# A graph layer with gathered rows: a window's rows of x transposed on chip, an explicit bound on each gather, and the first list and the final flag moved forward

## The chip, the cores and the metric

The kernel runs on one core of one Trainium2 chip. The metric is the device time of one execution in microseconds (us). Ten runs of the kernel before have a median of 24131.06 us. Five engines work side by side: PE (TensorE, matrix products), DVE (VectorE), ACT (ScalarE), POOL (GpSimd) and SP (SyncE). SP, ACT and POOL also issue DMA transfers.

## The reference

```python
src, dst = (edge_index[0], edge_index[1])
Xs = X[src]
m_data = Xs @ W_data.T + b_data
m_ctrl = Xs @ W_control.T + b_control
msg = jnp.where((edge_types == 0)[:, None], m_data, m_ctrl)
agg = jax.ops.segment_sum(msg, dst, num_segments=X.shape[0])
out = agg + (X @ W_self.T + b_self)
return jax.nn.relu(out)
...
x = _layernorm(x + _L0_gnn_ref(...), axis=-1)
```

There are 50,000 nodes with 128 features in float32 and 1,650,000 edges, sorted by their destination; each node has an edge to itself among them. An edge's type chooses one of two weight matrices. The output is the layer normalization, without scale or shift, of x plus the rectified sum.

## The kernel before

**Sums first, weights later.** Edges of one type with the same destination can be summed before the weights are applied. So the kernel sums rows of x by destination and type, and multiplies the sums with the weights once for each destination.

**Blocks.** The edges are cut into 503 blocks (`NBLK`), about 3,284 edges each. A block writes into a window of 112 nodes (`B`) that begins at a base read from the data. Most of its edges come as 24 chunks of 128 edges (2 steps `Q` with 12 chunks `R` each). Edges from a node to itself are left out of the chunks and their places are filled with other edges of the block (`fill`, L300 to L330, on DVE); such an edge's own row is added from the window's x, transposed (`left_out_rows`, L358 to L361). Another 128 edges of a block are fetched one row at a time (`single_rows`, L428 to L443).

**A block on the engines.** POOL gathers the 24 chunks: each is one indirect DMA of 128 rows of x (L464), six to a buffer and ten buffers (`SLOTS`). SP and ACT fetch the 128 single rows, 64 each in two batches of 32: an engine first loads 32 addresses into registers (L435) and then issues 32 DMAs of one row of 512 bytes (L440). DVE compares the edges' columns with 0 to 119 and so makes a matrix of ones and zeros for each chunk (`onehot`, L401) and counts them (L409). PE multiplies each chunk of rows with its matrix into a sum in PSUM (L483); after the twelfth chunk of a step it adds the single rows (L489), for which it waits once a block (`rows_fetched`, L446 to L451), and the counts for the bias (L492). DVE adds the step's result into the window's sums (L499) and begins the next window with the overlap (L512).

**The end of a block.** `layer` (L514) multiplies the window's x, transposed (`xT`), with the self weights (L517), and adds bias (L518) and weighted sums (L520), all into one PSUM tile `po`. `moments` (L523) takes the rectified `po` plus the window's rows of x (`xw`), then mean and variance on DVE. `root` (L532) is one square root on ACT, `store` (L537) normalizes and issues the output's DMA on SP (L543).

**Loads of the window.** Three blocks ahead, `window` (L390) loads the base of the block into a register of SP (L387) and loads the window's rows of x twice: as they are (`xw`, L393, 112 rows of 512 bytes) and transposed from a transposed copy in memory (`xT`, L395).

**Order.** The schedule is written out by hand: the loop at L566 goes over the blocks, and each engine's queue follows the order of its statements. `single_rows` is two blocks ahead (`AHEAD`), `fill` five (`RAHEAD`). Every ten blocks the next group's lists of edges are loaded (`load_edges`, L156 to L170). In a block SP's order is: the base, `xw`, `xT`, 32 addresses, 32 rows, the output of an earlier block, 32 addresses, 32 rows.

**Start and end.** The weights are loaded and transposed one after the other through two buffers (L905 to L911); after them `idx0`, the list for the first block's gathers, is loaded (L116). DVE copies the column numbers into PSUM (L127) before the list of ones (L130) from which POOL makes a triangle (L133). After the last block, DVE and PE work out from collected minima and maxima whether the data kept the assumptions of this path (L615 to L640); the flag is read by all engines, and a general path follows if it is set. With these inputs it is not set.

Of the kernel before, what the change touches and what calls it, by code (L numbers as in the profile page):

```python
# [11 lines left out]
F32 = mybir.dt.float32  # L12
# [4 lines left out]
ALU = mybir.AluOpType  # L17
AX = mybir.AxisListType
SP = mybir.EngineType.SP
# [3 lines left out]
N = 50000  # L23
D = 128
ROW = 4 * D
E = 1650000
P = 128
# [7 lines left out]
W = 60  # L35
Q = 2
PASS = 6
B = 112
C = R * Q
F = 42  # L40
S = 64
# [4 lines left out]
NBLK = 2 + (E - C * CH) // BE  # L46
# [7 lines left out]
AHEAD = 2  # L54
# [30 lines left out]
def straight(ctx, tc, c, x, x_t, src_t, dst_t, etype_t, src_f, dst_f, etype_f, src_x, dst_first, first_p, out):  # L85
# [13 lines left out]
    nc = tc.nc  # L99
    keep = ctx.enter_context(tc.tile_pool(name="keep", bufs=1))  # L100
# [6 lines left out]
    stp = ctx.enter_context(tc.tile_pool(name="stp", bufs=3))  # L107
# [3 lines left out]
    ps_o = ctx.enter_context(tc.tile_pool(name="ps_o", bufs=1, space=bass.MemoryType.PSUM))  # L111
# [7 lines left out]
    num = keep.tile([P, 2 * W], F32, name="num")  # L119
# [75 lines left out]
    base_i = keep.tile([1, BL], I32, name="base_i")  # L195
# [172 lines left out]
    def column(k):  # L368
        return k // R * R1 + k % R
# [11 lines left out]

    idxs = {0: idx0}
    bys, pcs, zs, pls, bases, ats, ys = {}, {}, {}, {}, {}, {}, {}
    ohs, cnts, accs, xws, xTs, pos, hs, mvs, sds = {}, {}, {}, {}, {}, {}, {}, {}, {}

    def base_of(b):
        return nc.values_load(base_i[0:1, b:b + 1], engines=[SP], min_val=0, max_val=N - B,  # L387
                              skip_runtime_bounds_check_because="it was clamped to this")

    def window(b):  # L390
        at = bases[b] = base_of(b)
        xw = stp.tile([B, D], F32, name="xw", bufs=5)
        nc.sync.dma_start(xw, x[bass.ds(at, B), :])  # L393
        xT = stp.tile([P, B], F32, name="xT", bufs=5)
        nc.sync.dma_start(xT, x_t[:, bass.ds(at, B)])  # L395
        xws[b], xTs[b] = xw, xT

    def onehot(b):
        g, i = divmod(b, GB)
# [13 lines left out]

    ROW_SLOTS = AHEAD + 2
    TURN = S // 2
    LOAD = TURN // 1
# [11 lines left out]
    def single_rows(b, q, part):  # L428

        if q == 0 and part == 0:  # L430
            ys[b] = stp.tile([S, Q, D], F32, name="yx", bufs=ROW_SLOTS)
        both = []
        for j, (eng, dma) in enumerate(((SP, nc.sync), (ACT, nc.scalar))):
            at = j * TURN + part * LOAD
            _, rows = nc.values_load_multi_w_load_instructions(  # L435
                ats[b][0:1, q * S + at:q * S + at + LOAD], engines=[eng], **RANGE)
            both.append([(dma, fetched[j][b % ROW_SLOTS], at + k, row) for k, row in enumerate(rows)])
        for pair in zip(*both):
            for dma, sem, k, row in pair:
                copy = dma.dma_start(ys[b][k:k + 1, q, :].bitcast(U8), x_bytes[:, bass.ds(row, ROW)])  # L440
# [17 lines left out]
    def gathers(b, ks):  # L458
        i = pass_no[0] % SLOTS
        pass_no[0] += 1  # L460
        y = gat.tile([P, PASS, D], F32, name="y")
        for k in ks:
            r = LAST if b == NBLK - 1 and k == RCH - 1 else P
            copy = nc.gpsimd.indirect_dma_start(  # L464
                out=y[:r, k % PASS, :], out_offset=None, in_=x,
                in_offset=bass.IndirectOffsetOnAxis(ap=idxs[b][:r, column(k):column(k) + 1], axis=0))
# [46 lines left out]

    def layer(b):  # L514
        a = sums[b % RING]
        po = ps_o.tile([B, D], F32, name="po")
        nc.tensor.matmul(po, xTs.pop(b), c["wselfT"], start=True, stop=False)  # L517
        nc.tensor.matmul(po, a[0:3, 2, :B], bias, start=False, stop=False)  # L518
        for t in range(2):
            nc.tensor.matmul(po, a[:, t, :B], c["wmsgT"][:, t * D:(t + 1) * D], start=False, stop=t == 1)  # L520
        pos[b] = po
# [15 lines left out]
    def store(b):  # L537
# [4 lines left out]
        nc.vector.tensor_scalar(o, hs.pop(b), mv[:, 0:1], rstd, op0=ALU.subtract, op1=ALU.mult)  # L542
        nc.sync.dma_start(out[bass.ds(bases.pop(b), B), :], o)  # L543

    for b in range(1, AHEAD + 1):
        offsets(b)
    columns(0)
# [6 lines left out]
    for b in range(1, RAHEAD):  # L554
        fill(b)
        left_out_columns(b)
        left_out_matrix(b)
        if b < AHEAD:
            onehot(b)
            counts(b)  # L560
            for q in range(Q):
                for part in range(1):
                    single_rows(b, q, part)
        if b == 1:
            clear_sums()
    for b in range(NBLK + 1):  # L566
        if b + 3 < NBLK:
            window(b + 3)
        g, i = divmod(b, GB)
# [11 lines left out]
        for q, (step, ks) in enumerate(passes_of(b)):  # L581
# [27 lines left out]
                left_out_matrix(b + RAHEAD)  # L609
                offsets(b + AHEAD + 1)  # L610
            if q % 2 == 0 and not plain(b + AHEAD):
                single_rows(b + AHEAD, q // 2, 0)


    ones = keep.tile([P, 1], F32, name="ones")  # L615
    nc.vector.memset(ones, 1.0)
    mm = keep.tile([P, 2], F32, name="mm")
    nc.vector.tensor_reduce(mm[:, 0:1], stats[:, :, 0, :], AX.XY, ALU.min)
    nc.vector.tensor_reduce(mm[:, 1:2], stats[:, :, 1, :], AX.XY, ALU.max)
    bad = keep.tile([P, 3], F32, name="bad")  # L620
    least = keep.tile([P, 1], F32, name="least")
    nc.vector.tensor_reduce(least, loops, AX.X, ALU.min)
    nc.vector.tensor_scalar(bad[:, 2:3], least, float(F), None, op0=ALU.is_lt)
    nc.vector.tensor_scalar(bad[:, 0:1], mm[:, 0:1], 0.0, None, op0=ALU.is_lt)
    nc.vector.tensor_scalar(bad[:, 1:2], mm[:, 1:2], float(W), None, op0=ALU.is_ge)
    gap = keep.tile([1, 3], F32, name="gap")
    nc.vector.tensor_reduce(gap[:, 0:1], shift, AX.X, ALU.min)
    nc.vector.tensor_reduce(gap[:, 1:2], shift, AX.X, ALU.max)
    nc.vector.tensor_scalar(gap[:, 0:1], gap[:, 0:1], 0.0, None, op0=ALU.is_lt)
    nc.vector.tensor_scalar(gap[:, 1:2], gap[:, 1:2], float(B), None, op0=ALU.is_gt)  # L630
    pb = ps_o.tile([B, D], F32, name="po")
    nc.tensor.matmul(pb[:3, 0:1], bad, ones, start=True, stop=True)
    both = keep.tile([3, 1], F32, name="both")
    nc.vector.tensor_copy(both, pb[:3, 0:1])
    pc = ps_o.tile([B, D], F32, name="po")
    nc.tensor.matmul(pc[:1, 0:1], both, ones[:3, 0:1], start=True, stop=True)
    nc.vector.tensor_copy(gap[:, 2:3], pc[:1, 0:1])
    total = keep.tile([1, 1], F32, name="total")
    nc.vector.tensor_reduce(total, gap, AX.X, ALU.add)
    nc.vector.tensor_copy(c["bad"], total)  # L640


def general(ctx, tc, c, x, src, dst, etype, out):
# [221 lines left out]
def gnn_resnorm(  # L865
# [109 lines left out]
```

## Time and profile before

| What | Value |
|---|---|
| Ten runs, median | 24131.06 us |
| Ten runs, lowest and highest | 24106.23 and 24138.2 us |
| Profiled execution, its own time | 24112.32 us |
| Profiled execution, span of its instructions | 24110.6 us |
| Busy share of the span | PE 29%, weight loads 26%, DVE 44%, ACT 1%, POOL 47% |
| DMA traffic | 970.58 MB in 753,406 packets, 40 GB/s on average |
| Issues | 32,064 single rows on SP and as many on ACT; 12,061 gathers on POOL; 503 each of `xw`, `xT` and the output on SP |

Busy times leave out the instructions that set registers, wait, or issue DMAs, so SP has no busy time of its own; its issues stand in the timeline as SPq, those of ACT as ACTq. A group's row in the profile gives line, engine, operation and tiles, then the number of instructions, the busy time in us, the mean of one in ns, and the engine's idle time just before them with what ended most of it. PEq is a wait in PE's sequencer.

### The profile page before, as it was taken

The page shows a single profiled execution, that of the slowest core. Times are in us where ns is not written, and L with a number is a line of the kernel's source. Part 1 is how long each engine was busy: PE and PEld are TensorE (multiplying, and loading weights), DVE is VectorE, ACT ScalarE, POOL GpSimd, SP SyncE. Part 2 cuts the span into 40 slices and gives each one's busy share as a digit, 9 for nine tenths or more (in the row PEclk, how much of TensorE's full clock was granted, in tenths as well). Part 3 has the DMA queues.
Part 4 walks back from the last instruction along what each step waited for, and adds up shares of the span by engine and source line. Part 5 has one row for each costly group of instructions (what it writes and reads, how often), then busy time and mean ns, then how long its engine had stood idle before and what let it go on. Part 6 is the DMA issues. An engine that isn't in the chain of part 4 may idle for free. (4 is left out here: it accounts for less than half of the span.)

```text
span 24110.6 us, 243274 instructions
## 1 busy us (share of the span) xinstructions
PE 7060.2 (29%) x34836; PEld 6353.7 (26%) x34837; DVE 10668.4 (44%) x13316; ACT 151.6 (1%) x509; POOL 11419.1 (47%) x12071
## 2 busy tenths in 40 slices
PE   2322322222232222322222222322223222232222
PEld 2222222222222222222222222222222222222222
DVE  5444444444444444444444444444444444444443
ACT  0000000000000000000000000000000000000000
POOL 5444444444444444444444444444444444444444
PEclk6555555555555555555555555555555555555555
DMA  1111111111111111111111111111111111111111
GB/s 44 41 41 39 40 41 41 39 40 41 40 40 40 41 40 40 40 40 41 39 41 40 41 40 40 40 40 40 40 40 41 40 40 41 40 40 41 41 39 37
DMA packets 753406, 970.58 MB, mean 40 GB/s; under 512 B 355316, under 2 KB 552099, under 8 KB 751778
## 3 DMA queue, kind: packets, MB, share of 16 engines
q0 software_dynamic: 385968, 791.19, 11.5%
q1 hardware_dynamic: 301244, 146.99, 2.3%
q10 hardware_dynamic: 64566, 16.74, 0.3%
q14 instruction: 1344, 11.01, 0.1%
q8 instruction: 284, 4.65, 0.1%
HBM read 924.76 MB, written 29.02 MB: 40 GB/s over the span
## 5 line engine op out<-in xcount | busy, mean ns | idle before, releaser
L464 POOL DMA_INDIRECT y<-in_x,idx x12048 | 11405.2, 947 | 12592.8 <-PE acc L483 7743.9
L499 DVE TENSOR_TENSOR sums<-acc,sums 128x180 f32 x1006 | 348.1, 346 | 11144.5 <-PE acc L492 10707.6
L483 PE MATMUL acc<-oh,y 128*128 128x120 f32 x24122 | 5098.2, 398 | 3.5 <-issue 3.5
L483 PEld LDWEIGHTS acc<-oh,y 128*128 128x128 f32 x24122 | 4860.5, 307 | 4.0 <-issue 4.0
L489 PE MATMUL acc<-oh,yx 64*128 64x120 f32 x2004 | 635.7, 408 | 11442.5 <-PEq L449 11301.1
L489 PEld LDWEIGHTS acc<-oh,yx 64*128 64x128 f32 x2004 | 401.7, 249 | 11632.5 <-PEq L449 11416.1
L409 DVE TENSOR_REDUCE cnt<-oh 128x240 bf16<-128x3120 f32 x503 | 2934.2, 5833 | 0.1
L401 DVE TENSOR_TENSOR oh<-col,small 128x3120 f32<-128x3120 f32 x503 | 1695.9, 3371 | 0.0
L336 PE MATMUL small<-ones_b,by 128*84 128x1 bf16 x501 | 115.9, 231 | 5319.4 <-DVE by L329 3157.5
L336 PEld LDWEIGHTS <-by 128*84 128x84 bf16 x501 | 73.3, 146 | 5386.9 <-DVE by L329 3197.1
L329 DVE TENSOR_REDUCE by<-old 128x84 bf16<-128x1092 f32 x501 | 1062.9, 2122 | 18.8 <-DVE old L326 1.4
L525 DVE SCALAR_TENSOR_TENSOR h<-po,xw 112x128 f32<-112x128 f32 x503 | 146.9, 292 | 1650.7 <-PE po L520 1470.0
L310 DVE TENSOR_TENSOR m<-rk,small 128x1092 f32<-128x1092 f32 x501 | 647.3, 1292 | 17.5 <-DVE small L308 0.5
L313 DVE TENSOR_TENSOR new<-m,small 128x1092 f32<-128x1092 f32 x501 | 647.0, 1291 | 17.2
L317 DVE TENSOR_REDUCE v_new<-new 128x26 f32<-128x1092 f32 x501 | 646.9, 1291 | 17.2
L326 DVE TENSOR_TENSOR old<-m,small 128x1092 f32<-128x1092 f32 x501 | 643.5, 1284 | 0.0
L520 PE MATMUL po<-wmsgT,sums 128*112 128x128 f32 x2012 | 525.6, 407 | 0.0
L520 PEld LDWEIGHTS po<-wmsgT,sums 128*112 128x112 f32 x2012 | 382.1, 261 | 110.7 <-issue 94.7
L518 PE MATMUL po<-bias,sums 3*112 3x128 f32 x1006 | 353.7, 448 | 9.8 <-DVE sums L499 8.0
L517 PE MATMUL po<-wselfT,xT 128*112 128x128 f32 x1006 | 315.5, 417 | 0.0
L534 ACT ACTIVATE sd<-mv,eps 112x1 f32<-112x1 f32 x503 | 148.3, 295 | 23768.2 <-issue 22066.2
L512 DVE TENSOR_TENSOR sums<-pl,sums 128x336 f32<-128x336 f32 x501 | 254.4, 508 | 84.6 <-issue 74.8
(115 smaller groups left out, 3673.3 us busy)
## 6 DMA issues: line engine op xcount, KB each, us to landing
yx<-in_x ACTq DMA_DIRECT2D x32064, 0.5 KB
yx<-in_x SPq DMA_DIRECT2D x32064, 0.5 KB
y<-in_x,idx POOLq DMA_INDIRECT x12048
xw<-in_x SPq DMA_DIRECT2D x503, 56.0 KB
xT<-in_x_t SPq DMA_DIRECT2D x503, 56.0 KB
out<-o SPq DMA_DIRECT2D x503, 56.0 KB
vf_all<-vd SPq DMA_DIRECT2D x51, 420.0 KB
s<-in_src_t SPq DMA_DIRECT2D x51, 130.0 KB
```

What stands on the lines that cost most here:

```text
L310: nc.vector.tensor_tensor(m, rk_g[g][:, i, :, None].to_broadcast([P, C1, F]), rank_no_ps[:, None, :].to_broadcast([P, C1, F]), op=ALU.is_e ...
L313: nc.vector.tensor_tensor(new.rearrange("p (q r) f -> p q r f", r=R1), m.rearrange("p (q r) f -> p q r f", r=R1), vf.rearrange("p (q f) -> ...
L317: nc.vector.tensor_reduce(v, new, AX.X, ALU.add)
L326: nc.vector.tensor_tensor(old, m, cb[:, :, None].to_broadcast([P, C1, F]), op=ALU.mult)
L329: nc.vector.tensor_reduce(by, old.rearrange("p (q r) f -> p q f r", r=R1), AX.X, ALU.add)
L401: nc.vector.tensor_tensor(oh, col_g[g][:, i, :, None].to_broadcast([P, C1, 2 * W]), num_ps[:, None, :].to_broadcast([P, C1, 2 * W]), op=AL ...
L409: nc.vector.tensor_reduce(cnt, ohs[b].rearrange("p (q r) w -> p q w r", r=R1), AX.X, ALU.add)
L464: copy = nc.gpsimd.indirect_dma_start(out=y[:r, k % PASS, :], out_offset=None, in_=x, in_offset=bass.IndirectOffsetOnAxis(ap=idxs[b][:r, c ...
L483: nc.tensor.matmul(acc[:, :2, :].rearrange("p t w -> p (t w)"), y[:r, k % PASS, :], ohs[b][:r, column(k), :], start=k == of_step[0], stop= ...
L489: nc.tensor.matmul(acc[:, :2, :].rearrange("p t w -> p (t w)"), ys[b][:, q, :], ohs[b][:S, q * R1 + R, :], start=False, stop=True)
L518: nc.tensor.matmul(po, a[0:3, 2, :B], bias, start=False, stop=False)
L520: nc.tensor.matmul(po, a[:, t, :B], c["wmsgT"][:, t * D:(t + 1) * D], start=False, stop=t == 1)
```

## The change

The window's rows of x are no longer loaded. PE transposes `xT` into the second half of the PSUM tile `po`, and DVE copies that half to `h` and adds the rectified half to it. SP loads the bases of five blocks at once. Each gather carries a bound for its indices, 49,999. The weights get three buffers in SBUF and PSUM each, and these SBUF buffers stay allocated. The copy of the column numbers stands after the list of ones and the triangle. The flag's work is moved ahead of the last block's. `single_rows` loses an argument that had one value only. Line numbers from L129 on shift by a few: the gather becomes L465, its product L485, the single rows L441, the row product L491, `xT`'s load L397, the transpose L520, the copy L530.

```diff
-    nc.vector.tensor_copy(num_ps, num)
 ...
     nc.gpsimd.affine_select(out=below, in_=ones_b, pattern=[[1, P]], compare_op=ALU.is_gt, fill=0.0,
                             base=0, channel_multiplier=-1)
+    nc.vector.tensor_copy(num_ps, num)
...
-    def base_of(b):
-        return nc.values_load(base_i[0:1, b:b + 1], engines=[SP], min_val=0, max_val=N - B,
-                              skip_runtime_bounds_check_because="it was clamped to this")
+    BASES = 5

     def window(b):
-        at = bases[b] = base_of(b)
-        xw = stp.tile([B, D], F32, name="xw", bufs=5)
-        nc.sync.dma_start(xw, x[bass.ds(at, B), :])
+        if b % BASES == 0:
+            n = min(BASES, NBLK - b)
+            _, regs = nc.values_load_multi_w_load_instructions(
+                base_i[0:1, b:b + n], engines=[SP], min_val=0, max_val=N - B,
+                skip_runtime_bounds_check_because="it was clamped to this")
+            bases.update({b + i: at for i, at in enumerate(regs)})
+        at = bases[b]
         xT = stp.tile([P, B], F32, name="xT", bufs=5)
         nc.sync.dma_start(xT, x_t[:, bass.ds(at, B)])
-        xws[b], xTs[b] = xw, xT
+        xTs[b] = xT
...
             copy = nc.gpsimd.indirect_dma_start(
                 out=y[:r, k % PASS, :], out_offset=None, in_=x,
-                in_offset=bass.IndirectOffsetOnAxis(ap=idxs[b][:r, column(k):column(k) + 1], axis=0))
+                in_offset=bass.IndirectOffsetOnAxis(ap=idxs[b][:r, column(k):column(k) + 1], axis=0),
+                bounds_check=N - 1)
...
     def layer(b):
         a = sums[b % RING]
-        po = ps_o.tile([B, D], F32, name="po")
-        nc.tensor.matmul(po, xTs.pop(b), c["wselfT"], start=True, stop=False)
+        both = ps_o.tile([B, 2, D], F32, name="po")
+        po, xT = both[:, 0, :], xTs.pop(b)
+        nc.tensor.transpose(both[:, 1, :], xT, c["ident"])
+        nc.tensor.matmul(po, xT, c["wselfT"], start=True, stop=False)
...
     def moments(b):
         h = stp.tile([B, D], F32, name="h")
-        nc.vector.scalar_tensor_tensor(h, pos.pop(b), 0.0, xws.pop(b), op0=ALU.max, op1=ALU.add)
+        po = pos.pop(b)
+        nc.vector.tensor_copy(h, po[:, 1, :])
+        nc.vector.scalar_tensor_tensor(h, po[:, 0, :], 0.0, h, op0=ALU.max, op1=ALU.add)
...
     for b in range(NBLK + 1):
+        if b == NBLK - 1:
+            find_bad()
...
-    with tc.tile_pool(name="wts", bufs=2) as wts, \
-            tc.tile_pool(name="wts_ps", bufs=2, space=bass.MemoryType.PSUM) as wts_ps:
-        for w, o in ((w_data, wmsgT[:, :D]), (w_ctrl, wmsgT[:, D:]), (w_self, wselfT)):
-            w_sb = wts.tile([P, D], F32, name="w_sb")
+    w_all = const.tile([P, 3, D], F32, name="w_all")
+    with tc.tile_pool(name="wts_ps", bufs=3, space=bass.MemoryType.PSUM) as wts_ps:
+        for i, (w, o) in enumerate(((w_data, wmsgT[:, :D]), (w_ctrl, wmsgT[:, D:]), (w_self, wselfT))):
+            w_sb = w_all[:, i, :]
```

`find_bad` is the block of statements of L615 to L640 as a function, with its two small products in the first half of a `po` tile.

More of the change, by code (lines that the diff above doesn't have):

```diff
@@ L383, in straight @@
     bys, pcs, zs, pls, bases, ats, ys = {}, {}, {}, {}, {}, {}, {}
-    ohs, cnts, accs, xws, xTs, pos, hs, mvs, sds = {}, {}, {}, {}, {}, {}, {}, {}, {}
-    def base_of(b):
-        return nc.values_load(base_i[0:1, b:b + 1], engines=[SP], min_val=0, max_val=N - B,
-                              skip_runtime_bounds_check_because="it was clamped to this")
+    ohs, cnts, accs, xTs, pos, hs, mvs, sds = {}, {}, {}, {}, {}, {}, {}, {}
+    BASES = 5
     def window(b):
-        at = bases[b] = base_of(b)
-        xw = stp.tile([B, D], F32, name="xw", bufs=5)
-        nc.sync.dma_start(xw, x[bass.ds(at, B), :])
+        if b % BASES == 0:
[5 more added lines that the diff above has]
+        at = bases[b]
         xT = stp.tile([P, B], F32, name="xT", bufs=5)
         nc.sync.dma_start(xT, x_t[:, bass.ds(at, B)])
-        xws[b], xTs[b] = xw, xT
+        xTs[b] = xT
     def onehot(b):
@@ L415, in straight @@
     TURN = S // 2
-    LOAD = TURN // 1
     RANGE = dict(min_val=0, max_val=(N - 1) * ROW, skip_runtime_bounds_check_because="where a node's row is")
@@ L426, in offsets, with single_rows @@
             nc.vector.tensor_scalar(ats[b], one_g[g][:, i * X:(i + 1) * X], float(ROW), None, op0=ALU.mult)
-    def single_rows(b, q, part):
-        if q == 0 and part == 0:
+    def single_rows(b, q):
+        if q == 0:
             ys[b] = stp.tile([S, Q, D], F32, name="yx", bufs=ROW_SLOTS)
@@ L433, in single_rows @@
         for j, (eng, dma) in enumerate(((SP, nc.sync), (ACT, nc.scalar))):
-            at = j * TURN + part * LOAD
+            at = j * TURN
             _, rows = nc.values_load_multi_w_load_instructions(
-                ats[b][0:1, q * S + at:q * S + at + LOAD], engines=[eng], **RANGE)
+                ats[b][0:1, q * S + at:q * S + at + TURN], engines=[eng], **RANGE)
             both.append([(dma, fetched[j][b % ROW_SLOTS], at + k, row) for k, row in enumerate(rows)])
@@ L520, in layer @@
             nc.tensor.matmul(po, a[:, t, :B], c["wmsgT"][:, t * D:(t + 1) * D], start=False, stop=t == 1)
-        pos[b] = po
+        pos[b] = both
     def moments(b):
         h = stp.tile([B, D], F32, name="h")
-        nc.vector.scalar_tensor_tensor(h, pos.pop(b), 0.0, xws.pop(b), op0=ALU.max, op1=ALU.add)
+        po = pos.pop(b)
+        nc.vector.tensor_copy(h, po[:, 1, :])
+        nc.vector.scalar_tensor_tensor(h, po[:, 0, :], 0.0, h, op0=ALU.max, op1=ALU.add)
         st = stp.tile([B, 6], F32, name="st")
@@ L543, in store, with find_bad @@
         nc.sync.dma_start(out[bass.ds(bases.pop(b), B), :], o)
+    def find_bad():
+        ones = keep.tile([P, 1], F32, name="ones")
+        nc.vector.memset(ones, 1.0)
+        mm = keep.tile([P, 2], F32, name="mm")
+        nc.vector.tensor_reduce(mm[:, 0:1], stats[:, :, 0, :], AX.XY, ALU.min)
+        nc.vector.tensor_reduce(mm[:, 1:2], stats[:, :, 1, :], AX.XY, ALU.max)
+        bad = keep.tile([P, 3], F32, name="bad")
+        least = keep.tile([P, 1], F32, name="least")
+        nc.vector.tensor_reduce(least, loops, AX.X, ALU.min)
+        nc.vector.tensor_scalar(bad[:, 2:3], least, float(F), None, op0=ALU.is_lt)
+        nc.vector.tensor_scalar(bad[:, 0:1], mm[:, 0:1], 0.0, None, op0=ALU.is_lt)
+        nc.vector.tensor_scalar(bad[:, 1:2], mm[:, 1:2], float(W), None, op0=ALU.is_ge)
+        gap = keep.tile([1, 3], F32, name="gap")
+        nc.vector.tensor_reduce(gap[:, 0:1], shift, AX.X, ALU.min)
+        nc.vector.tensor_reduce(gap[:, 1:2], shift, AX.X, ALU.max)
+        nc.vector.tensor_scalar(gap[:, 0:1], gap[:, 0:1], 0.0, None, op0=ALU.is_lt)
+        nc.vector.tensor_scalar(gap[:, 1:2], gap[:, 1:2], float(B), None, op0=ALU.is_gt)
+        pb = ps_o.tile([B, 2, D], F32, name="po")[:, 0, :]
+        nc.tensor.matmul(pb[:3, 0:1], bad, ones, start=True, stop=True)
+        both = keep.tile([3, 1], F32, name="both")
+        nc.vector.tensor_copy(both, pb[:3, 0:1])
+        pc = ps_o.tile([B, 2, D], F32, name="po")[:, 0, :]
+        nc.tensor.matmul(pc[:1, 0:1], both, ones[:3, 0:1], start=True, stop=True)
+        nc.vector.tensor_copy(gap[:, 2:3], pc[:1, 0:1])
+        total = keep.tile([1, 1], F32, name="total")
+        nc.vector.tensor_reduce(total, gap, AX.X, ALU.add)
+        nc.vector.tensor_copy(c["bad"], total)
     for b in range(1, AHEAD + 1):
@@ L561, in straight @@
             for q in range(Q):
-                for part in range(1):
-                    single_rows(b, q, part)
+                single_rows(b, q)
         if b == 1:
@@ L611, in straight @@
             if q % 2 == 0 and not plain(b + AHEAD):
[L612 to L640, printed above, removed]
+                single_rows(b + AHEAD, q // 2)
 def general(ctx, tc, c, x, src, dst, etype, out):
```

## The prediction

> **What bounds the kernel now.** I read the engines' shares first (the page's first part), then the longest idle times among the costly groups, then SyncE's own waits, then SyncE's order of time.
>
> ```profile
> PE 7060.2 (29%) x34836; PEld 6353.7 (26%) x34837; DVE 10668.4 (44%) x13316; ACT 151.6 (1%) x509; POOL 11419.1 (47%) x12071
> ...
> L464 POOL DMA_INDIRECT y<-in_x,idx x12048 | 11405.2, 947 | 12592.8 <-PE acc L483 7743.9
> ...
> L489 PE MATMUL acc<-oh,yx 64*128 64x120 f32 x2004 | 635.7, 408 | 11442.5 <-PEq L449 11301.1
> ```
>
> No engine is busy half of the time. PE stands still 11,301 us in front of L489, and what ends that is L449, its wait for the single rows of x that SP and ACT fetch (L440). The gathers in turn wait for PE to free a buffer. So everything waits for the single rows. SP's waits are next (us in total, times, longest):
>
> ```profile
> SPq L435 <- DVE sums L499: 445.3, 402, 1.9
> SPq L292 <- DVE cb L273: 15.2, 1, 15.2
> ```
>
> Under 2% of the span: SP waits for nobody, it is always issuing. Its order of time over one block in the middle, and over a block at the end, where no gather is left:
>
> ```profile
> 12001.35 0.32 SPq L393 DMA_DIRECT2D xw<-in_x  x1
> 12001.86 0.36 SPq L395 DMA_DIRECT2D xT<-in_x_t  x1
> 12004.56 22.19 SPq L440 DMA_DIRECT2D yx<-in_x  x32
> 12028.23 0.02 SPq L543 DMA_DIRECT2D out<-o  x1
> 12030.42 18.98 SPq L440 DMA_DIRECT2D yx<-in_x  x32
> 12050.34 0.32 SPq L393 DMA_DIRECT2D xw<-in_x  x1
> ...
> 24054.15 0.32 SPq L393 DMA_DIRECT2D xw<-in_x  x1
> 24054.65 0.36 SPq L395 DMA_DIRECT2D xT<-in_x_t  x1
> 24057.05 10.68 SPq L440 DMA_DIRECT2D yx<-in_x  x32
> 24067.99 0.34 SPq L543 DMA_DIRECT2D out<-o  x1
> 24070.57 10.24 SPq L440 DMA_DIRECT2D yx<-in_x  x32
> 24081.08 15.10 SPq L543 DMA_DIRECT2D out<-o  x4
> ```
>
> The same 32 issues take 22.2 and 19.0 us beside gathers and 10.7 and 10.2 us without. L393 runs 503 times from 28.7 to 24054.0 us: a block takes 47.86 us. The block without gathers takes 24081.08 - 24054.15 = 26.9 us, plus 0.54 for the base load (L387) that this stretch lacks: 27.5 us. So SP's instructions alone are 27.5 us of a block, and the 24 gathers of a block cost SP 20.4 us in stalls. A gather starts every 1.25 us in a run (12006.14, 12007.39, 12008.65), 30.0 us in a block: SP loses 0.68 us for each us in which POOL gathers. ACT, with as many rows, has slack: its load for the first rows starts at 12019.31, 10.7 us after its last issue, when DVE has made the offsets.
>
> A rule of the Trainium skill speaks against this reading and against the change: "DMA: Bandwidth & Descriptors", section "Issuing engines are not separate DMA queues", says that what a sequencer spends on starting DMAs is usually small beside the transfers. By it, an issue less on SP is worth nothing, and the sum below would be -6 us. Here the row differs: the software queue holds 11.5% of the DMA engines and SP's queue 2.3%, while SP issues without a pause. I follow the row.
>
> **The change part by part.**
>
> SP, per block. The xw load goes: one L393 DMA, its address and its register move. What the trace answers for the two lines (durations in ns: least, median, most):
>
> ```profile
> L393 SPq FUSED_REGOPS  x503: 3/37/1397, 28.7 to 24054.0; - x168
> L393 SPq MOVE xw<-in_x x503: 3/29/726, 28.8 to 24054.1; - x168
> L393 SPq DMA_DIRECT2D xw<-in_x x503: 3/322/737, 29.0 to 24054.2; - x168
> ...
> L387 SPq TENSOR_LOAD <-base_i x503: 3/539/1422, 28.3 to 24053.4; - x168
> ```
>
> From xw's issue to xT's is 0.50 us in both places shown; I take 0.50. The base load goes in four blocks of five. The fifth loads five values: 32 values (L435) take 1.868 us and one takes 0.539, so 0.043 for each more, 0.71 us for five. Saved: (503 x 0.54 - 101 x 0.71)/503 = 0.40 us. Together 0.90 us unhindered. Some of these meet stalls (maxima of 1.4 us against a median of 0.04 to 0.54), so 0.90 is a low side and about 1.15 the high one; I take 1.0. All of it is on the path, since SP never waits: 503 x 1.0 = -503 us. SP also gets 144 more semaphore instructions (1,219 against 1,075 in the built programs, 17 ns each in the rows): 2 us in all. They are waits for transfers issued blocks before, so I cost them at nothing; were they late, each would hold the rows queued behind it.
>
> PE. One transpose a block, ahead of L517's product, same operand: half of L517's two records, 0.42 us. It delays the six products behind the layer, whose end frees the buffer for the block's second run of gathers; POOL's 2.90 us gap there (2.8 to 2.9 in every block that I looked at, ended by po L520) becomes about 3.3. That moves gathers, it adds none, and POOL stands still another 15 to 17 us before the next block's first. Nothing; if POOL were the bound, 503 x 0.42 = 211 us.
>
> DVE. A copy of 112x128 out of PSUM, like L525 with 0.292 us, put between the layer and L525, which loses its wait on xw's DMA. Behind it stand the moments, the next one-hot (L401) and the counts; then DVE waits 22 to 24 us for PE at L499. Hidden there; uncovered it would be 503 x 0.32 = 161 us.
>
> POOL. Each gather now carries its bound in a register: 12,061 register moves, one ahead of each gather, and a comparison inside. The trace of before has neither.
> - The move: nearest row L440's MOVE, 29 ns, 0.06 us to the next start. POOL's own semaphore instructions (17 ns) stand between gathers, and the gap stays 0.30 us with one as without; in the rows some of them run before the gather ahead has ended. Bounds 0 and 0.06 us; I take 0.01, nearer the row of the same engine. 24 x 0.01 x 0.68 = 0.16 us a block, +82 us.
> - The comparison: nearest row L464 itself, 947 ns for 128 indices, 7.4 ns each. No page of the skill states a price. If it is done for many indices at once, nothing; if it adds a tenth per index, 0.095 us a gather, 24 x 0.095 x 0.68 = 1.55 us a block, +780 us; a fifth, +1,560. A gain isn't excluded either, should the unbounded form take a longer way: -0.05 us would be -410. I take 0, since the 947 ns hardly vary (941 to 947 up to the median) and look like set-up more than like a loop over indices, and keep the other ends.
>
> The gathers keep their addresses and their bytes, so their stalls of SP stay.
>
> Once-only parts. The weights get three buffers of their own, so the first list (SP's L116, issued at 6.01 us behind the weights' loads and transposes) goes out at about 1 us, and all of SP's start with it: -5 us. DVE's copy of num goes behind the list of ones: it waited 5.4 us for POOL's iota, at the same start, and is inside these 5. The flag's 3.0 us of DVE (L616 to L640, 24095.76 to 24098.78) go ahead of the last block, where DVE waited 3.82 us in one place and 18 in another; the last products may then start a us later, and the tail after the last store loses up to 3: -1 us.
>
> Sum: the profiled execution took 24112.3 us (span 24110.6). 24112.3 - 503 + 82 - 6 = 23,685. The median of the ten runs is 18.8 us above the profiled one, so 23,704; I say 23,700 (-1.8%).
>
> **The rivals.**
>
> The bound costs time inside the gather, and it is slower. Place: L465 on POOL, 24 times a block. From 0.061 us a gather (1.0 / (24 x 0.68)) it eats all that SP saves. At a tenth of 947 ns the time is 23,700 - 82 + 780 = 24,400, at a fifth 25,180. For it: 24 of them a block, in the unit that sets SP's stalls, and 7.4 ns for an index leaves no room for a scalar comparison. Against it: longer pauses between transfers might let SP through more often, so that 0.68 is too much; at half of it, 24,010 for a tenth.
>
> The stalls take what is freed. If a block's time is set by what the gathers and rows occupy together and not by SP's own instructions, 0.9 us less of SP's work is filled with stalls: no change, 24,125. For it: SP and ACT are held at the same times. Against it: ACT, held as much, still has 10.7 us to spare, and the block without gathers falls to 27.5 us.
>
> The gain is larger: a gather with a bound is shorter by 0.05 us, or 56 KB less to fetch per block thins the stalls: 23,300. For it nothing but that no row excludes it.
>
> **How the numbers follow.** The forecast has 0.58, with 23,550 to 23,850 as its own range (0.7 to 1.2 us a block, the move between 0 and 0.02 us). The dearer gather has 0.29: 0.01 that it eats only part of the gain, 0.02 that it just cancels it, 0.26 that it costs more, a third of that beyond 24,650. The stalls that fill up have 0.05 (0.03 no change, 0.02 a little slower by the gathers' moves), the larger gain 0.08. Leaving out the far end of the dear gather and part of the larger gain, the range is 23,350 to 24,650. About 0.2%, 48 us, is what a measurement of this kernel can tell from no change. Faster: 0.58 + 0.08 + 0.01 = 0.67. Same: 0.02 + 0.03 = 0.05. Slower: 0.26 + 0.02 = 0.28.
>
> **What would show it.** Right: the period of the xT issue (L397) near 46.9 us; PE's idle time before the row product still ended by its wait for single rows, some 500 us less; the gather at 947 ns, 1.25 to 1.26 us from start to start. Wrong: a gather group with a mean over 1,010 ns; a gap between gathers over 0.30 us by more than the move; SP batches that last longer than 19 to 22 us; SP waiting in front of xT or out; POOL or DVE without their long waits for PE.

## The result, and the profile after

The changed kernel takes 23331.82 us in the median, the kernel before, run beside it, 24126.78 us. The ratio is 0.9672, 95% interval [0.9664, 0.9681]: 795 us less, or 1.58 us for each of 503 blocks. The time lies 18 us below the low end of the predicted range, 23,350, and 372 us below the 23,704 of the prediction's sum.

Runs were taken in sets, each with the kernel before beside the changed ones. The kernel before took 23,795 to 24,127 us (medians) in some sets and 15,119 to 15,147 us in others, and a kernel is compared only with the runs of before in its own set. The comparison above, and the profile that the prediction was made from, belong to the long ones; I call them stalled sets, for a reason that the timelines show.

The lines of the page after that answer to those shown of before:

```profile
PE 6996.6 (30%) x35339; PEld 6307.2 (27%) x35340; DVE 10832.6 (46%) x13819; ACT 151.4 (1%) x509; POOL 12219.5 (52%) x12071
...
L465 POOL DMA_INDIRECT y<-in_x,idx x12048 | 12204.8, 1013 | 11046.5 <-PE acc L485 6570.7
...
L491 PE MATMUL acc<-oh,yx 64*128 64x120 f32 x2004 | 633.9, 406 | 10699.0 <-PEq L450 10667.1
```

The gather has become longer, 1013 ns against 947: 12,048 of them are 800 us more of POOL. And yet PE's idle time in front of the row product, still ended by its wait for the single rows, is 634 us less (11,301 to 10,667). What bound the kernel still does, but PE waits less for it. SP's own waits (us in total, times, longest) are 0.65 us a block, where the 445 us of before were 0.89:

```profile
SPq L436 <- DVE sums L501: 328.2, 194, 2.3
SPq L292 <- DVE cb L273: 15.4, 1, 15.4
```

For the rest SP is still issuing. Its order of time in the middle and at the end:

```profile
12021.69 0.36 SPq L397 DMA_DIRECT2D xT<-in_x_t  x1
12024.26 20.62 SPq L441 DMA_DIRECT2D yx<-in_x  x32
12045.59 0.00 SPq L549 DMA_DIRECT2D out<-o  x1
12047.78 19.57 SPq L441 DMA_DIRECT2D yx<-in_x  x32
12068.36 0.36 SPq L397 DMA_DIRECT2D xT<-in_x_t  x1
...
23296.15 0.36 SPq L397 DMA_DIRECT2D xT<-in_x_t  x1
23298.74 10.58 SPq L441 DMA_DIRECT2D yx<-in_x  x32
23309.57 0.34 SPq L549 DMA_DIRECT2D out<-o  x1
23312.16 10.25 SPq L441 DMA_DIRECT2D yx<-in_x  x32
23322.69 17.70 SPq L549 DMA_DIRECT2D out<-o  x4
```

The 503 issues of `xT` run from 24.8 to 23296.2 us: a block takes 46.36 us, where it was 47.86. The last block, which has no gather beside it, takes 26.54 us from `xT` to the last stores, and a fifth of the load of five bases (1.327 us in the median) belongs to it: 26.8 us of SP's own work, against 27.5. So 0.7 of the 1.5 us are SP's own work as such a block shows it. What a block takes beyond that (stalls, the short waits, and a tenth of the loads that come every ten blocks) is 20.4 us before and 19.6 now, although POOL gathers longer.

Two or three batches of a timeline are a small sample: single batches of 32 rows take from 10 to over 50 us. So I also worked out the mean over all 1,002 batches of SP in each trace, from the start of the first row's issue to the end of the last one's. It is 19.73 us before and 19.89 now. The rows themselves have not become faster; what has become shorter is the rest of SP's block, 47.86 - 2 x 19.73 = 8.4 us before and 46.36 - 2 x 19.89 = 6.6 now.

POOL's own order of time:

```profile
12044.94 1.01 POOL L465 DMA_INDIRECT y<-in_x,idx  x1 [2.14 <-PE po L524]
12046.26 1.01 POOL L465 DMA_INDIRECT y<-in_x,idx  x1 [0.30 <-issue]
12047.58 1.01 POOL L465 DMA_INDIRECT y<-in_x,idx  x1 [0.30 <-issue]
```

A gather now starts every 1.32 us instead of every 1.25. The gap of 0.30 us is unchanged; what has grown is the gather itself.

### The profile page after: what moved, and what is told of

Read it like the earlier page. It is cut to its first block, busy times and chain, and to the rows that moved or that the text cites. A ratio compares the mean times of both kernels' runs of the same rounds, so it can differ in the third digit from the quotient of the medians.

```text
span 23346.2 us, 254666 instructions
## 1 busy us (share of the span) xinstructions
PE 6996.6 (30%) x35339; PEld 6307.2 (27%) x35340; DVE 10832.6 (46%) x13819; ACT 151.4 (1%) x509; POOL 12219.5 (52%) x12071
## 4 chain that ended last, share of the span: by engine, by line
SPq 55%; issue 34%; DVE 6%; PE 3%; DMA 2%; another core or an unknown queue 0%; ACTq 0%; PEldq 0%; DVEq 0%; ACT 0%
SPq L441 46%; SPq L436 6%; DVE cnt L411 2%; DMA yx<-in_x 2%; SPq L549 2%; PE acc L485 1%; PE acc L491 1%; SPq L397 0%; DVE m L310 0%; DVE new L313 0%; DVE v_new L317 0%; DVE old L326 0%; PE po L524 0%; DVE by L329 0%
## 5 line engine op out<-in xcount | busy, mean ns | idle before, releaser
L465 POOL DMA_INDIRECT y<-in_x,idx x12048 | 12204.8, 1013 | 11046.5 <-PE acc L485 6570.7
L485 PE MATMUL acc<-oh,y 128*128 128x120 f32 x24122 | 4983.3, 391 | 13.2 <-issue 13.1
L485 PEld LDWEIGHTS acc<-oh,y 128*128 128x128 f32 x24122 | 4740.7, 300 | 11.2 <-issue 10.9
L491 PE MATMUL acc<-oh,yx 64*128 64x120 f32 x2004 | 633.9, 406 | 10699.0 <-PEq L450 10667.1
L491 PEld LDWEIGHTS acc<-oh,yx 64*128 64x128 f32 x2004 | 402.4, 249 | 10876.9 <-PEq L450 10774.7
L530 DVE COPY h<-po 112x128 f32<-112x128 f32 x503 | 146.8, 292 | 1806.2 <-PE po L524 1644.7
```

The costliest lines, as they stand in the source:

```text
L465: copy = nc.gpsimd.indirect_dma_start(out=y[:r, k % PASS, :], out_offset=None, in_=x, in_offset=bass.IndirectOffsetOnAxis(ap=idxs[b][:r, c ...
L485: nc.tensor.matmul(acc[:, :2, :].rearrange("p t w -> p (t w)"), y[:r, k % PASS, :], ohs[b][:r, column(k), :], start=k == of_step[0], stop= ...
L491: nc.tensor.matmul(acc[:, :2, :].rearrange("p t w -> p (t w)"), ys[b][:, q, :], ohs[b][:S, q * R1 + R, :], start=False, stop=True)
```

## The experiments

Two accounts of the gain were set against each other: SP's saved instructions, as the prediction had it, and the bound, which makes a gather longer and might let SP's issues pass.

### Parts of the change, first set (not a stalled one)

`e1`: before, with the bound alone. `e2`: after, without it. `e3`: before, with PE's transpose in the place of the `xw` load. `e4`: before, with the bases of five blocks loaded at once. Excerpts of the edits (`...` stands for lines not shown):

```diff
 e1, against before
+                bounds_check=N - 1)
 e2, against after
-                bounds_check=N - 1)
 e3, against before
-        xw = stp.tile([B, D], F32, name="xw", bufs=5)
-        nc.sync.dma_start(xw, x[bass.ds(at, B), :])
+        nc.tensor.transpose(both[:, 1, :], xT, c["ident"])
+        nc.vector.tensor_copy(h, po[:, 1, :])
 ...
 e4, against before
-        at = bases[b] = base_of(b)
+        if b % 5 == 0:
 ...
```

> The kernel before with nothing but the bound on each gather. If SP loses 0.68 us for each us in which POOL gathers, as the prediction had it, a gather of 1013 ns instead of 947 costs 24 x 0.066 x 0.68 = 1.08 us a block: 24,670. If the stalls go with the number of gathers and not with their length, nothing: 24,127 within 0.3%. If slower gathers let SP and ACT through more often, so that the bound itself is a part of the gain: below 24,050, at most by the 300 us that SP's own savings do not explain (23,830).

> The changed kernel without the bound on the gathers (947 ns each expected). Stall by POOL's time: 23,332 - 540 = 22,790. Stall by the number of gathers: 23,330. Bound as a part of the gain: about 23,630.

> The kernel before with PE's transpose in place of the load of xw, and nothing else: bases are still loaded one by one, no bound. By SP's issue time alone, 0.5 to 0.7 us a block: 23,775 to 23,875. If the load's 112 rows of 512 bytes also hindered the single rows, more than that: 1.0 us a block or more, below 23,620.

> The kernel before with the bases of five blocks loaded at once, and nothing else. By SP's issue time 0.4 us a block: 23,925. In the changed kernel the load of five takes 1.33 us and not the 0.71 that the prediction had, which leaves 0.54 - 1.33/5 = 0.27 us a block: 23,990.

| Kernel | us | Ratio to before in the same set |
|---|---|---|
| before | 15147.07 | |
| e1, bound alone | 15932.16 | 1.0519 [1.0501, 1.0536] |
| e2, all but the bound | 15133.36 | 0.9991 [0.9982, 1.0001] |
| e3, transpose alone | 15144.48 | 0.9999 [0.9989, 1.0008] |
| e4, bases alone | 15147.87 | 1.0001 [0.9991, 1.0011] |

In this set before was 9 ms faster than where the prediction was made. The page of `e3` (the engines' shares of the chain that ended last, and its gathers) and its orders of time on SP and POOL show why; the last line is the gather of `e1`:

```profile
POOL 56%; issue 20%; PE 11%; DVE 7%; DMA 6%; ACTq 1%; POOLq 0%; PEldq 0%; ACT 0%; DVEq 0%; SPq 0%
...
L462 POOL DMA_INDIRECT y<-in_x,idx x12048 | 11385.2, 945 | 3682.8 <-issue 3566.6
...
L464 POOL DMA_INDIRECT y<-in_x,idx x12048 | 12175.8, 1011 | 3677.8 <-issue 3649.7
```

```profile
8008.39 10.27 SPq L438 DMA_DIRECT2D yx<-in_x  x32
8021.71 0.34 SPq L545 DMA_DIRECT2D out<-o  x1
8024.64 10.19 SPq L438 DMA_DIRECT2D yx<-in_x  x32
```

```profile
8008.67 0.94 POOL L462 DMA_INDIRECT y<-in_x,idx  x1 [0.30 <-issue]
8009.92 0.94 POOL L462 DMA_INDIRECT y<-in_x,idx  x1 [0.30 <-issue]
```

The gathers run at 1.25 us as they did, but 32 rows take 10.2 to 10.3 us on SP beside them, as long as in the block without gathers (10.47 us in the mean over the trace). So nothing stalls SP here, POOL is the bound, and the time is 503 x 24 x 1.25 = 15,090 us plus the ends. Then each part costs what POOL's row says: with the bound a gather starts every 1.316 us, 1.316 / 1.25 = 1.053 times as long, and the kernel takes 1.0519 times as long; what is saved on SP is worth nothing. That is what the prediction had drawn from the Trainium skill's "DMA: Bandwidth & Descriptors", section "Issuing engines are not separate DMA queues", and left. It comes true here because POOL is the bound, not because issuing is small: two batches are 21 of SP's 30 us. But these four don't say where the 795 us came from.

### The changed kernel again, and the parts once more

`e5` is the changed kernel as it is.

> The changed kernel itself, once more. Where SP's issues are stalled as in the first traces: 0.967 of the kernel before. On a chip where they are not, POOL's gathers are the bound; there the bound on its own cost 5.2% and the rest of the change nothing, so 1.05.

23328.17 against 24112.96 us, 0.9672 [0.9655, 0.9688]: a stalled set, and the first ratio again. The parts were repeated on the same chip: `e6` is e1, `e7` is e2, `e8` is e3.

> The kernel before with nothing but the bound, on a chip where SP's issues are stalled beside gathers (e1 ran on one where they are not). Stall by POOL's time: 1.08 us a block more, 24,670. Stall by the number of gathers: 24,113 within 0.3%. Slower gathers let SP and ACT through: below 24,040, towards 23,830. If chip 11 comes again: 1.05.

> The changed kernel without the bound, on a stalled chip. Stall by POOL's time: 22,790. Stall by the number of gathers: 23,330. Slower gathers let SP and ACT through: about 23,630. If chip 11 comes again: 0.999.

> The kernel before with PE's transpose in place of the load of xw and nothing else, on a stalled chip. SP's issue time alone, 0.5 to 0.7 us a block: 23,760 to 23,860. If the load's 112 rows also hinder the single rows: 1.0 us or more, below 23,610. If chip 11 comes again: 1.000.

| Kernel | us | Ratio |
|---|---|---|
| before | 15119.01 | |
| e6, bound alone | 15904.63 | 1.0519 [1.0502, 1.0537] |
| e7, all but the bound | 15106.56 | 0.9991 [0.9982, 1.0001] |
| e8, transpose alone | 15116.78 | 0.9998 [0.9989, 1.0008] |

The same chip was stalled in one set and not in the next, so it isn't the chip alone that decides. In the same set ran `e9`, the changed kernel with 28 of a step's 64 rows on SP and 36 on ACT, in two loads of 18 (excerpt):

```diff
-    TURN = S // 2
+    N_SP = 28
...
+        for j, eng, dma, at, n in ((0, SP, nc.sync, 0, N_SP), (1, ACT, nc.scalar, N_SP, (S - N_SP) // 2),
+                                   (1, ACT, nc.scalar, (S + N_SP) // 2, (S - N_SP) // 2)):
```

> The changed kernel with 28 of a batch's 64 single rows on SP and 36 on ACT (in two loads of 18 addresses) in place of 32 and 32. If SP's own instructions are the bound and the stalls go with the gathers, SP has 8 rows a block less, 8 x 0.32 = 2.6 us: 22,000, if a row takes its stall with it, 8 x 0.63 = 5 us: 20,800. If what all queues issue together is the bound, SP's share doesn't matter: 23,330. If chip 11 comes again: 1.05, as POOL's gathers are the bound there.

18596.99 us, 1.2303 [1.2282, 1.2323]. The rows of ACT delay the square root that ends a block:

```profile
L544 DVE RECIPROCAL rstd<-sd 112x1 f32<-112x1 f32 x503 | 82.4, 164 | 5670.5 <-ACT sd L538 5670.5
```

DVE stands still 5,670 us for ACT's `sd` alone, which is queued behind ACT's issues; with 32 rows each (`e1`, before with the bound) it is 9.9 us. The rows moved to ACT became a new bound, and since this set wasn't stalled the run says nothing of the prediction's steps.

### The bound alone in a stalled set

> The kernel before with nothing but the bound, in a set of runs of its own, as e5 was, where the kernel before took 24,113 us; the sets of four had it at 15,119 to 15,147 us, on the same chip too. If such a set of one brings the stalls back: stall by POOL's time 24,670; stall by the number of gathers 24,113 within 0.3%; slower gathers let SP and ACT through: below 24,040, towards 23,830. If not: 15,904, 1.052 of the kernel before.

`e10` is e1 again: 23099.23 against 23801.38 us, 0.9704 [0.9688, 0.972]. The same edit that costs 5.2% where SP isn't stalled gains 3.0% where it is. Its gathers, SP and POOL:

```profile
L464 POOL DMA_INDIRECT y<-in_x,idx x12048 | 12173.7, 1010 | 10816.2 <-PE acc L484 6415.7
```

```profile
12000.50 19.44 SPq L440 DMA_DIRECT2D yx<-in_x  x32
12020.72 0.32 SPq L393 DMA_DIRECT2D xw<-in_x  x1
12021.22 0.36 SPq L395 DMA_DIRECT2D xT<-in_x_t  x1
12023.62 19.07 SPq L440 DMA_DIRECT2D yx<-in_x  x32
```

SP has all its instructions of before, `xw` among them, and a batch of its rows takes 19.15 us in the mean of 1,002, where the trace of before, from another set, has 19.73. A block takes 45.8 us (503 issues of `xT`, 29.8 to 23043.3 us), of which 27.5 are SP's own: what comes on top fell from 20.4 to 18.3 us.

### The rest, and a pause too short to change the pace

`e11` is e2 again, all but the bound. `e12` asks whether any other instruction on POOL does the same: before, with a small memset behind each gather.

```diff
+    pause = keep.tile([P, 1], F32, name="pause")
...
             tc.add_to_no_dep_group(f"rows{b}_{ks[0]}", copy.ins)
+            nc.gpsimd.memset(pause, 0.0)
```

> The changed kernel without the bound, in a set where SP's issues are stalled. The bound alone gave 0.970 there (e10) and the whole change 0.967 (e5), so the rest of the change is worth 0.3%: 0.997. If SP's saved issue time counted by itself (1.0 us a block), 0.979. If the stalls don't come back in this set: 0.999.

> The kernel before, without the bound, with a small memset (128x1) on POOL after each gather. If it is the pace of the gathers that lets SP and ACT through, it must not matter what slows them: with 0.1 to 0.2 us more from one gather to the next the time falls by more than with the bound's 0.066 us, to 0.90 to 0.96. If it is the bound itself (a gather of another kind for the queues), the pause gives no gain: 1.00, or 1.02 and more by POOL's time. If the stalls don't come back in this set: 24 x 0.15 us a block more on POOL, 1.08 to 1.16.

Before took 23794.72 us beside them. `e11`: 23513.22, 0.9893 [0.9877, 0.991]. `e12`: 24107.46, 1.0135 [1.0118, 1.0152]. POOL in `e12`:

```profile
12013.03 0.94 POOL L466 DMA_INDIRECT y<-in_x,idx  x1 [0.19 <-issue]
12013.98 0.11 POOL L472 MEMSET pause<- 128x1 f32 x1
12014.28 0.94 POOL L466 DMA_INDIRECT y<-in_x,idx  x1 [0.19 <-issue]
```

The memset fits into the 0.30 us gap, a gather still starts every 1.25 us, and nothing is gained. So an instruction more on POOL isn't enough. That it lost 1.35% was not expected and is not explained: in its trace the gathers' pace and SP's batches (19.75 us in the mean) are those of before.

This gives a scale for stalled sets. An edit that leaves the pace as it was moved the time by 1.35%, and before itself differs by 1.4% from set to set, though a kernel repeats within 0.7% inside a set. A difference below some 1.4% can't be put down to one part of the change with certainty; the 3.0% of `e10` and all that follows with longer pauses lie above it. Measured against `e12` in place of before, `e11` gained 2.5%.

### Pauses that change the pace

The same edit with 256 and 640 columns instead of one: 0.33 us (`e13`) and 0.65 us (`e14`) of memset.

> The kernel before, without the bound, with a memset of 128x256 on POOL after each gather, about 0.3 us, so that a gather starts every 1.3 to 1.4 us. If the pace lets SP and ACT through: 0.93 to 0.97, as or better than with the bound (1.316 us, 0.970). If it is the bound itself: 1.01 to 1.05, since POOL gathers longer.

> The same with a memset of 128x640, about 0.55 us, so that a gather starts every 1.55 to 1.7 us. If the pace lets SP and ACT through, further down, 0.82 to 0.92, until POOL itself is the bound (24 x 1.6 = 38.4 us a block, 0.81). If it is the bound itself: 1.1 and more by the prediction's 0.68 us a us.

Not a stalled set (before 15120.16 us): 17442.22 us, 1.1535 [1.1516, 1.1555], and 21310.21 us, 1.4094 [1.407, 1.4117]. A gather starts every 1.44 and 1.76 us, 1.15 and 1.41 times 1.25: POOL is the bound and the pause is simply added. `e15` is e13 again:

> The kernel before, without the bound, with a memset of 128x256 after each gather: a gather starts every 1.44 us (from e13, where POOL was the bound with 24 x 1.44 = 34.7 us a block, 17,442 us). Where SP's issues are stalled: if the pace lets SP and ACT through, well below the bound's 0.970, to 0.80 to 0.93, with 17,442 us as the floor; if it is the bound itself, 1.05 and more. If the stalls don't come back: 1.15.

Stalled: 19850.9 against 24099.69 us, 0.8232 [0.8219, 0.8246]. POOL and SP in `e15`, and its row product:

```profile
12030.36 0.95 POOL L466 DMA_INDIRECT y<-in_x,idx  x1 [0.17 <-issue]
12031.31 0.33 POOL L472 MEMSET pause<- 128x256 f32 x1
12031.80 0.95 POOL L466 DMA_INDIRECT y<-in_x,idx  x1 [0.17 <-issue]
```

```profile
12008.88 14.11 SPq L440 DMA_DIRECT2D yx<-in_x  x32
12023.78 0.32 SPq L393 DMA_DIRECT2D xw<-in_x  x1
12024.33 0.36 SPq L395 DMA_DIRECT2D xT<-in_x_t  x1
12026.73 11.71 SPq L440 DMA_DIRECT2D yx<-in_x  x32
12038.79 0.26 SPq L546 DMA_DIRECT2D out<-o  x1
12041.29 10.70 SPq L440 DMA_DIRECT2D yx<-in_x  x32
12052.76 0.32 SPq L393 DMA_DIRECT2D xw<-in_x  x1
12053.90 0.02 SPq L395 DMA_DIRECT2D xT<-in_x_t  x1
12055.71 23.51 SPq L440 DMA_DIRECT2D yx<-in_x  x32
```

```profile
L492 PE MATMUL acc<-oh,yx 64*128 64x120 f32 x2004 | 631.2, 406 | 7200.4 <-PEq L449 4337.6
```

The gathers are those of before, without a bound, of the same rows and bytes, 953 ns each. Only their pace differs. SP's batches still vary, here from 10.7 to 23.5 us, but their mean over the trace falls from 19.73 to 16.08 us; PE's wait for single rows falls from 11,301 to 4,338 us. A block takes 39.5 us, of which 27.5 are SP's own: 12.0 us come on top, where before had 20.4.

### The transpose alone in a stalled set

> The kernel before with PE's transpose in place of the load of xw, and nothing else, in a set of its own. By SP's issue time, 0.5 to 0.7 us of 47.9: 0.985 to 0.990. If the freed time fills up with stalls and the 1.1% of e11 come from the bases: 1.00. If the load's rows also hinder the single rows: below 0.985. If the stalls don't come back: 1.000.

`e16` is e3 again: 23685.73 against 23821.05 us, 0.9943 [0.9927, 0.996], or 135 us: 0.27 us a block for a load that the prediction put at 0.50. By the scale above, 0.6% is too little to lean on.

### A pause in the place of the bound

The changed kernel, the bound taken away, and a memset of 340 columns (0.40 us) behind each gather: a gather every 1.51 us (`e17`; excerpt, against after).

```diff
+    pause = keep.tile([P, 340], F32, name="pause")
...
-                bounds_check=N - 1)
...
+            nc.gpsimd.memset(pause, 0.0)
```

> The changed kernel with a memset of 128x340 on POOL after each gather in place of the bound: by the pauses of e13 and e14 a gather starts every 1.51 us, and POOL's floor is 503 x 24 x 1.51 = 18,230 us. Where SP's issues are stalled: below e15's 0.823, about 0.77 to 0.80; with SP's saved issue time counting again in full, close to the floor of 0.76. If the stalls don't come back: POOL is the bound, 1.21.

> The kernel of e17 again. Where SP's issues are stalled: 18,309 us, as where they are not, is the floor (0.76 of 24,100); e15, with a gather every 1.44 us and without the rest of the change, had 0.823. If the two gains add up, 0.77 to 0.80; if SP's saved time is filled with stalls, 0.80 to 0.82. If the stalls don't come back: 1.21.

`e17` met a set that wasn't stalled: 18308.76 against 15147.54 us, 1.2087 [1.2066, 1.2107]. `e18`, the same kernel, met a stalled one: 18319.66 against 24090.87 us, 0.7606 [0.7594, 0.7619]. The engines' shares of the chain that ended last in `e18`, and its gathers:

```profile
POOL 69%; issue 15%; DVE 8%; PE 3%; SPq 2%; another core or an unknown queue 1%; PEld 1%; DMA 1%; POOLq 0%; DVEq 0%; PEldq 0%; ACT 0%; ACTq 0%
...
L467 POOL DMA_INDIRECT y<-in_x,idx x12048 | 11495.2, 954 | 1983.6 <-issue 1967.8
```

SP has 2% of the chain and POOL carries it: 503 x 24 x 1.51 = 18,229 us plus the ends, in both sets alike. SP's batches take 14.74 us in the mean, still not the 10.5 of a set without stalls, but they no longer decide. In a stalled set this version beats both kernels, by 24% and (18,320 against 23,332, in different sets) by 21%; in the others it is 21% slower than before.

## Why the prediction was right or wrong

**The step that failed: "SP loses 0.68 us for each us in which POOL gathers".** It divided one block's stalls by one block's gathers and took the quotient for a slope, so that more POOL time had to mean more stalls. The runs show that the time falls instead:

| Stalled sets: kernel | From gather to gather, us | Ratio to before in its set |
|---|---|---|
| e12, short pause | 1.25 | 1.0135 |
| e10, bound | 1.316 | 0.9704 |
| e15, pause | 1.44 | 0.8232 |
| e18, pause, no `xw` load, bases of five | 1.51 | 0.7606 |

More POOL time doesn't stall SP more; gathers that follow each other less closely stall it less. `e15` shows this without the bound: the pause alone takes 8.4 us of stalls from a block. Its gathers keep their addresses and their bytes, from which the prediction had concluded that their stalls of SP stay. For the bound, the pace is the likely account and not a shown one: its pace lies between and so does its gain, at about half of what a straight line from 1.25 to 1.44 us gives (0.970 against 0.939). Two things keep it open. A pause of just 1.316 us wasn't run, so a further effect of the bound on SP isn't excluded. And the pauses also widen the gap between two gathers (0.30 us to 0.49 in `e15` and 0.56 in `e18`), which the bound leaves as it was, so gap and pace aren't told apart by them. The prediction had the thought that longer intervals might let SP through, as a reason why 0.68 might be too much; it halved the loss with it and did not ask whether the sign holds.

**The comparison inside the gather: 0, with ends -0.05 and +0.19 us.** It is 1013 - 947 = 66 ns, inside the ends, and 0.5 ns an index: 7.4 ns an index did leave room for it. By the prediction's own rate it would have cost 0.066 x 24 x 0.68 x 503 = 540 us. It cost nothing in the stalled sets; on its own it gained 3.0%, 714 us of 24,127. The size was bounded well and the sign of its price wrong.

**SP's saved work: 1.0 us a block, -503 us.** The two loads' sum came out about right in the two profiles: from the end of SP's previous issue to the end of its own, `xw` took 0.70 us a block and the base load 0.59, now 0.23, which is 1.06 us less. But that the freed time shows in full isn't settled. `e11`, with all the parts but the bound, gained 1.07% [0.9, 1.23] on before in its set: about 255 us, 0.5 us a block, half; on `e12` in the same set it gained 594 us, 1.2 us a block. In a block without gathers SP's own work fell by 0.7 us, not 0.9; the load of five bases takes 1.327 us in the median, where a straight line between one value and 32 gave 0.71:

```profile
L391 SPq TENSOR_LOAD <-base_i x101: 163/1327/1442, 23.9 to 23214.1; - x101
```

If `e11` against before is the right measure, half of what was freed was filled with stalls, as the rival with a chance of 0.05 would have it for all. Bases alone weren't run in a stalled set, nor the parts at start and end. "SP never waits" was not exact either: its 445 us of waits for DVE are 0.9 us a block, as much as the saving that was counted. They were 599 us in `e16` and 328 in the changed kernel. And its ends of 0.7 to 1.2 us a block, with moves of 0 to 0.02 us, give 23,521 to 23,937 by its own sum, where it wrote 23,550 to 23,850; the result lies below both.

**Where the 795 us lie.** They can't be divided with certainty. The two halves of the change don't add: 0.9704 x 0.9893 = 0.960, against 0.9672 for both. By ratios, the bound on top of all the rest is worth 0.9672 / 0.9893 = 0.978, 540 us; by times, 23,513 - 23,332 = 181 us. These come from different sets, in which before itself differed by 1.4%. The traces show little of such a gain:

| Trace, stalled | Mean batch of 32 rows on SP, us | Rest of SP's block, us |
|---|---|---|
| before | 19.73 | 8.4 |
| after | 19.89 | 6.6 |
| e11, after without the bound | 19.92 | 6.6 |
| e10, before with the bound | 19.15 | 7.5 |
| e15, before with the pause | 16.08 | 7.3 |

In the changed kernel the rows take as long with the bound as without it; only in `e10`, with the instructions of before, do they come out faster with it. What the profiles of before and after show is a block shorter by 1.5 us: 1.06 us less in the two loads, as priced, some 0.8 less in SP's other instructions and waits, which the prediction did not count, and 0.3 us more in the rows, although POOL gathers 1.6 us longer and the rate of 0.68 asked for 1.1. So of the 372 us between 23,704 and 23,332, 82 are the priced register moves that cost nothing; how much of the rest is the bound and how much SP's own saving stays open.

**The register move: 0.01 us a gather, +82 us.** The 12,061 moves take 29 ns and are hidden; the gap between gathers stays 0.30 us. The price was zero, and the rate that it was multiplied with was the failed one.

```profile
L465 POOLq MOVE  x12061: 29/29/29, 1.2 to 23274.9; - x198
```

**What held.** SP bound the kernel and PE waited for single rows, before and after. The transpose takes 421 ns on PE and the copy 292 ns on DVE, as put. The first gather starts at 3.23 us instead of 8.09, 4.9 us earlier, where 5 were predicted. POOL's gap behind `po` did not grow to 3.3 us as forecast: it fell from 2.9 to 2.2 in the mean, hidden in both cases.

**The rivals.** The dearer bound was real in its place (1013 ns against the 1,010 that the prediction named as its sign) and would have decided, slower by 5%, where SP isn't stalled. That the direction came out right owes something to luck: with the measured 66 ns at its own rate the sum would have been 23,704 + 540 = 24,244 us, slower than before. Two errors, a term taken as nothing and a price with the wrong sign, hid each other. The larger gain came near in time, 23,300, but for reasons that weren't so: it wanted a shorter gather, or thinner stalls by 56 KB less, and `e16`, which drops these 56 KB alone, gained 0.6%.

## What to carry to other kernels

A stall divided by what runs beside it is an average; before it prices an edit as a slope, ask in which direction the edit moves the other side, and try one deliberate pause. Where one engine's issues are stalled beside another's stream of gathers and the second has time to spare, a longer interval between gathers can be worth more than any instruction saved, up to the interval at which the paced engine becomes the bound (here SP still held the kernel of before at 1.44 us, and POOL the changed one at 1.51). Run before again in every set: the same edit was worth -3% and +5%, and the set decided which. And run an edit that should do nothing, to see how large a difference means something.

## What the runs showed of the hardware that was not expected

- SP's issue of a one-row DMA beside gathers of 128 rows comes in two conditions. In one, 32 rows take 10.5 us in the mean with gathers at every 1.25 us (`e3`), and before takes 15.1 ms; in the other they take 19.7 us and before takes 24 ms. One chip showed both, and so did one kernel, on different chips (`e17`, `e18`). The transfers are not what differs: the gathers' packets fill 11.5% of the 16 DMA engines in 24,111 us before and 17.8% in 15,901 us in `e1`, 2,770 and 2,830 us, and a gather takes POOL 947 and 945 ns (before, `e3`). What decides the condition is open, and so is what holds the issues up behind SP.
- In the stalled condition the issue is very sensitive to the gathers' pace: 15% more from gather to gather (1.25 to 1.44 us) took away 8.4 of 20.4 us of stalls in a block.
- A memset of 0.11 us between two gathers is free for POOL, inside the gap of 0.30 us; one of 0.33 us adds 0.19 us to the pace.
- A bound on a gather of 128 indices adds 66 ns, whatever the condition (1011 ns in `e1`, 1010 in `e10`, 1013 in the changed kernel).
